# Graph attention with residual norm: the order of the last tiles' powers and stores, the last tile's normalisation, and twelve more stored residuals

## The chip, the cores and the metric

The kernel runs on one core of a Trainium2 chip. The metric is the device time of one execution, in microseconds; lower is better.

## The reference

For 16 batches of 1024 rows of 512 float32 values, the reference computes masked attention with eight heads, adds the input, and normalises every row:

```python
q = (x @ Wq + bq).reshape(b, n, H, HD)          # likewise k, v
scores = jnp.einsum('bqhd,bkhd->bhqk', q, k) / jnp.sqrt(jnp.float32(HD))
scores = scores + (1.0 - adj)[None, None, :, :] * -1000000000.0
attn = jax.nn.softmax(scores, axis=-1)
out = jnp.einsum('bhqk,bkhd->bqhd', attn, v).reshape(b, n, d)
y = x + out @ Wo + bo
result = (y - mean(y)) / sqrt(var(y) + 1e-5)    # over the last axis
```

The adjacency is the same for all batches and sparse: most rows have only a few keys. Rows without any key attend evenly to all of them.

## The kernel before

**Tiles.** Rows are ranked by their number of keys and taken in tiles of 128 rows, eight tiles (`t` from 0 to 7) for a batch `b`; a tile's number is 8b + t. `OWN` gives the number of keys that a tile handles one by one, one *block* for each: 2, 1, 2, 3, 4, 5, 5, 7. Tile 4 of each batch is thus the four-key tile. Rows with more keys than that (tiles 6 and 7) have further blocks, which are added up by a matmul (`add_up`). A block gathers one row of keys and values for each of the 128 queries (`kvg`, an indirect DMA on the queue of GpSimd, which the profile calls POOL), multiplies and reduces on VectorE (DVE), takes exponentials on ScalarE (ACT) and weighs the values on ACT or DVE.

**The schedule.** The program is written out block by block by a planner in Python, in the order in which each engine then works through it. `now[0]` is the step, one for each block. `later(k, fn)` puts a piece of work into the plan of the step k further on, `later_last(k, fn)` into the rest of that step, which comes behind the plan. TensorE (PE) work is paced by a credit: the projections of coming batches (`fronts`) while there are any, and the output products (`finish`) of tiles that are done. `total` is the number of blocks; the steps from `total` on only finish tiles. Each engine, and the DMA queue of each issuing engine (SP issues the plain DMAs), works strictly in the order written.

**A tile's x.** `load_x` gathers the tile's rows of x on POOL (L1010) into one of three buffers; PE transposes them, and the function `out` in `transpose_x` copies the result. For a tile whose number is in `STORED`, SP then writes the gathered rows to a DRAM tensor `residual` (L773), and the load of the tile three further on, which takes the same buffer, is put off by two steps. At the end of a tile, `load_y` needs x again: for a stored tile SP reads `residual` (L1035), for another POOL gathers it once more (L1038).

**The end of a tile.** When its last block is done, `normalise` (DVE) divides by the sum of the exponentials, and `turn` has PE transpose the tile; ACT copies it to `OT` (L1390). `finish` adds the output bias `bo_bc` to y on DVE (L1076), or, in the body of the program for spilled tiles, has a small matmul add it, and has PE do the output product (L799). `complete` then does, in this order: the sum y + product with its row sum (DVE, L1113), the sum of squares about the mean (`spread`, ACT, L1120), `variance` (DVE, L1123), `power`, the inverse square root (POOL, L1126; for two tiles at once L1160), `shift` (DVE, L1129), `norm_out` (ACT, L1134) and `store`, an indirect DMA on POOL (L1138). In the body two tiles share one power instruction, and their steps are put several steps apart. A product that comes back in the last three steps is held until step `total`. In a tile that ends at `total` - 1 or later (`ending`), all the steps follow at once:

```python
            later_last(0 if ending else 1, spread)
            if ending:
                for step in (variance, power, shift):
                    later(1, step)
                later_last(1, norm_out)
```

and `norm_out` puts `store` two steps on with `later(2, store)`. The last tile, `closes[total - 1]`, is tile 6 of batch 15. A pair whose second tile comes in step s has its two shifts and its first `norm_out` in s + 6 and its second `norm_out` in s + 7.

At the very end each engine reads a flag (L1608), which says whether a general version of the kernel has to run in addition; with these inputs it doesn't.

Of the kernel before, what the change touches and what calls it, by code (L numbers as in the profile page):

```python
# [14 lines left out]
OP = mybir.AluOpType  # L15
# [27 lines left out]
LAZY = 2  # L43

SPILL = (*(8 * b + t for b in range(4, 12) for t in (3, 6)), 45, 69, 93, 102, 103, 106, 107)
STORED = {*SPILL, *(i for i in range(10, 102) if i % 8 in (2, 5, 7)), *(i for i in range(102, 128) if i % 8 > 1)}
LATE = 12

AHEAD_LAST = 11
# [129 lines left out]
def kernel(  # L179
# [36 lines left out]
    nc = tc.nc  # L216
    B, N, D = x.shape
# [28 lines left out]
    bo_bc = const.tile([P, D], F32, name="bo_bc")  # L246
# [8 lines left out]
    with ExitStack() as main:  # L255
# [6 lines left out]
        def fill_psum(name):  # L262
            return psum.tile([P, HALF], F32, tag="fill", name=name, bufs=4)
# [80 lines left out]
        def number(b, t):  # L344
            return b * NT + t if t < NT else -1
# [4 lines left out]
        spill = {i: dram.tile([P, D], F32, name=f"spill_{i}") for i in SPILL}  # L350
        residual = {i: dram.tile([P, D], F32, name=f"residual_{i}") for i in sorted(STORED)}
        zeros = work.tile([P, D + HEADS], F32, tag="pv0", name="zeros", bufs=3)
# [93 lines left out]
        now, plan, rest, urgent, known, waiting, combined = [0], {}, {}, [], [], [], []  # L446

        def later(k, fn):
            plan.setdefault(now[0] + k, []).append(fn)

        def later_last(k, fn):
            rest.setdefault(now[0] + k, []).append(fn)
# [170 lines left out]
        shifts, looked = [], []  # L623
# [114 lines left out]
        X, XT, SX, KV, VSUM, NRM, Y, OT, PS = {}, {}, {}, {}, {}, {}, {}, {}, {}  # L738
# [13 lines left out]
        def transpose_x(b, t):  # L752
            def pe():
# [5 lines left out]
                def out():  # L759
# [3 lines left out]
                    if t == 0 and b >= PAIRED_FROM:  # L763
# [7 lines left out]
                        nc.scalar.activation(sq[0:LONE, :], xs[0:LONE, :], AF.Square, accum_out=x_norm[0:LONE, b:b + 1])  # L771
                    if b * NT + t in STORED:
                        nc.sync.dma_start(residual[b * NT + t], xs)  # L773
# [251 lines left out]
        def load_y(b, t, k=None):  # L1025
# [7 lines left out]
            loaded[b, t] = now[0]  # L1033
            if number(b, t) in STORED:
                nc.sync.dma_start(Y[b, t], residual[b * NT + t])  # L1035
# [32 lines left out]
        def finish(b, t):  # L1068


            mean_row = t == ONE_KEY and b >= PAIRED_FROM
            plain = bool(fronts) or mean_row
            biased = not plain and now[0] < total and number(b, t) in (*SPILL, -1)

            if not plain and not biased:
                nc.vector.tensor_tensor(Y[b, t], Y[b, t], bo_bc, op=OP.add)  # L1076

            def out(p):
                OT.pop((b, t))
                if mean_row:  # L1080
                    keep_mean(b, p)
                if not fronts and total - 4 < now[0] < total:
                    later(total - now[0], lambda: complete(b, t, p, plain))
                else:
                    complete(b, t, p, plain)

            units = product(f"po_{b}_{t}", lambda c: OT[b, t][:, ts(c, P)], W["o"], out)
            if biased:
                def bias():
                    nc.tensor.matmul(  # L1090
                        PS[f"po_{b}_{t}"], three.to_broadcast([P, P]), bo_3, start=False, stop=False
                    )

                units.insert(2, (BIAS, bias, None))
            return units

        def complete(b, t, p, plain):
            n, rows, offset = rows_of(b, t)
            y, p = Y[b, t][0:n, :], p[0:n, :]
            ending = not fronts and now[0] >= total - 1  # L1100
            single = fronts or ending or n < P
            if single:
                st = small.tile([P, 5], F32, name="stats", bufs=6)[0:n, :]
            else:

                second = bool(half)
                if not second:
                    half.append([small.tile([P, 2, 5], F32, name="stats_2", bufs=5)])
                st2 = half[0][0]
                st = st2[:, int(second), :]  # L1110
            if plain:
                nc.vector.tensor_tensor(y, p, y, op=OP.add)
            nc.vector.scalar_tensor_tensor(  # L1113
                y, bo_bc[0:n, :] if plain else p, 1.0, y, op0=OP.mult, op1=OP.add, accum_out=st[:, 0:1]
            )

            def spread():

                sq = work.tile([P, D], F32, tag="ysq", name=f"ysq_{b}_{t}", bufs=1)
                nc.scalar.activation(sq[0:n, :], y, AF.Square, bias=st[:, 0:1], scale=-float(D), accum_out=st[:, 2:3])  # L1120

            def variance():
                nc.vector.tensor_scalar(st[:, 2:3], st[:, 2:3], 1.0 / D ** 3, EPS, op0=OP.mult, op1=OP.add)  # L1123

            def power():
                nc.gpsimd.tensor_tensor(st[:, 3:4], st[:, 2:3], neg_half[0:n, :], op=OP.pow)  # L1126

            def shift():
                nc.vector.scalar_tensor_tensor(  # L1129
                    st[:, 4:5], st[:, 0:1], -1.0 / D, st[:, 3:4], op0=OP.mult, op1=OP.mult  # L1130
                )

            def norm_out():
                nc.scalar.activation(y, y, AF.Identity, bias=st[:, 4:5], scale=st[:, 3:4])  # L1134
                later(2, store)

            def store():
                nc.gpsimd.indirect_dma_start(  # L1138
                    out=out_rows[b, t], out_offset=bass.IndirectOffsetOnAxis(ap=rows, axis=0),
                    in_=y, in_offset=None, element_offset=offset,  # L1140
                )
                del Y[b, t]

            later_last(0 if ending else 1, spread)
            if ending:
                for step in (variance, power, shift):
                    later(1, step)
                later_last(1, norm_out)
            elif single:
                late = 1 if fronts else 0  # L1150
                later(2 + late, variance)
                later(3 + late, power)
                later(4 + 2 * late, shift)
                later_last(5 + 2 * late, norm_out)
            elif second:
                later(3, variance)
                mate_shift, mate_norm_out = half.pop()[1]

                def powers():
                    nc.gpsimd.tensor_tensor(  # L1160
                        st2[:, :, 3:4], st2[:, :, 2:3], neg_half[:, :, None].to_broadcast([P, 2, 1]), op=OP.pow
                    )

                def shifts():
                    mate_shift()
                    shift()

                later(4, powers)
                later(6, shifts)
                later_last(6, mate_norm_out)  # L1170
                later_last(7, norm_out)
            else:
                later(3, variance)
                mine = half[0]
                mine.append((shift, norm_out))

                def alone():
                    if half and half[0] is mine:
                        half.pop()
                        power()  # L1180
                        later(2, shift)
                        later_last(3, norm_out)

                later(6, alone)
# [34 lines left out]
        closes = {n: tile_closed for tile_closed, n in closing.items()}  # L1219
# [162 lines left out]
        def turn(b, t, o):  # L1382
            def transpose():
                p = fill_psum(f"poT_{b}_{t}")
                for c in range(NPAIR):
                    nc.tensor.transpose(p[:, ts(c, P)], o[:, ts(c, P)], ident)  # L1386

                def out():
                    OT[b, t] = work.tile([P, D], F32, tag="oT", name=f"oT_{b}_{t}", bufs=LAZY + 2)
                    nc.scalar.copy(OT[b, t], p)  # L1390
                    if number(b, t) in SPILL:
                        later(1, lambda: nc.sync.dma_start(spill[b * NT + t], OT.pop((b, t))))
                        spilled.append((b, t))
                    else:
                        later(1, lambda: done.append((b, t)))

                later(1, out)

            later(1, lambda: urgent.append(transpose))
            if not fronts:  # L1400
                coming.append((b, t))
# [65 lines left out]
        done, coming, spilled, gathered, fronts, guarded = [], [], [], [0], [], []  # L1467

        total = len(blocks)
# [29 lines left out]
        with tc.manual_schedule():  # L1499
# [21 lines left out]
            while n < total or plan or rest or urgent or done or finishing or spilled or lone_tiles or not guarded:  # L1521
# [6 lines left out]
                elif n in start:  # L1528

                    b = start.index(n)  # L1530
# [110 lines left out]
```

## Time and profile before

| | |
|---|---|
| median of 3 runs | 1849.95 us (1849.7 to 1851.8) |
| the profiled execution | 1851.61 us, span 1849.8 us |
| granted TensorE clock, mean | 0.994 |
| busy: PE, DVE, ACT, POOL | 97%, 91%, 85%, 68% |
| DMA | 555.39 MB, mean 300 GB/s |
| residual stores and reads on SP | 71 and 71 |
| gathers of y on POOL (L1038) | 58, 64.1 us busy |
| stores of the output on POOL (L1138) | 129, 150.5 us busy |

The durations in the profile come from one execution, whose own time is some 1.7 us above the median. A line names an instruction by engine, line of the kernel and operation, then output and input. POOLq and SPq are the queues that issue DMAs; "idle before" is the time in which the engine had nothing to do before an instruction, with what released it, where "issue" means that nothing shown held it. The spans on POOL are rough, and a DMA instruction on POOL stands for the work of issuing it, not for the transfer.

### The profile page before, as it was taken

To read this page: it belongs to the slowest core of one execution; us is meant where nothing else is said; L and a number is where in the kernel's file an instruction comes from. 1 tells how busy PE (TensorE), PEld (TensorE's weight loads), DVE (VectorE), ACT (ScalarE), POOL (GpSimd) and SP (SyncE) were. 2 spreads that over 40 slices of the span, in tenths; PEclk is the share of its full clock that TensorE was granted. 3 is DMA by queue.
4 is the path that set the end of the run, shared out by engine and by line. 5 is a ranking of instruction groups with operands and counts; after the bars stand their busy time and mean duration, and the time that the engine had idled before them with its cause. 6 is when DMAs were issued, how large, how long until landed. Compare 5 with 4: busy or idle time off the path is not lost.

```text
span 1849.8 us, 25305 instructions
## 1 busy us (share of the span) xinstructions
PE 1800.1 (97%) x5127; PEld 874.5 (47%) x5140; DVE 1691.9 (91%) x3472; ACT 1565.2 (85%) x6184; POOL 1249.1 (68%) x1154
## 2 busy tenths in 40 slices
PE   7999999999999999999999999999999999999996
PEld 3444454554444454454444445444444444444442
DVE  6889889999989999999999999999999999997885
ACT  3637869989889898999899988999799999977786
POOL 1367866777676686767667676677666777666785
PEclk9999999999999999999999999999999999999998
DMA  7357797988888999989989998998989899898984
GB/s 286 111 186 241 250 326 247 333 303 313 314 285 301 306 319 316 354 302 311 330 311 315 347 311 280 340 327 305 353 304 326 314 347 330 314 326 311 341 312 162
DMA packets 196295, 555.39 MB, mean 300 GB/s; under 512 B 33258, under 2 KB 33278, under 8 KB 196130
## 3 DMA queue, kind: packets, MB, share of 16 engines
q0 software_dynamic: 113600, 373.64, 59.6%
q1 hardware_dynamic: 79454, 174.23, 25.0%
q10 hardware_dynamic: 3076, 5.82, 0.9%
q14 instruction: 122, 1.00, 0.2%
q8 instruction: 43, 0.70, 0.2%
HBM read 420.30 MB, written 154.30 MB: 311 GB/s over the span
## 4 chain that ended last, share of the span: by engine, by line
PE 72%; DVE 11%; DMA 5%; ACT 4%; issue 3%; POOL 1%; SPq 0%; POOLq 0%; DVEq 0%; ACTq 0%
PE po L799 17%; PE pq L799 15%; PE pp L956 13%; PE z L956 9%; PE x L956 9%; ACT pv L1326 2%; PE pxT L757 2%; DVE qk L1298 2%; PE poT L1386 2%; DVE s L1302 2%; PE sum L1352 2%; PE sum L1351 2%; DMA kvg<-kv_pair,place_row 2%; DVE pv L1342 1%; DMA oTs<-spill 1%
## 5 line engine op out<-in xcount | busy, mean ns | idle before, releaser
L1326 ACT ACTIVATE pv<-kvg,pv 128x64 f32<-128x64 f32 x3600 | 907.1, 340 | 0.0
L1277 POOL DMA_INDIRECT kvg<-kv_pair,place_row x462 | 532.2, 1152 | 289.0 <-ACT pv L1326 89.8
L799 PE MATMUL pq<-wq,xT 128*128 128x512 f32 x792 | 368.2, 596 | 0.9 <-DVE q L830 0.9
L1302 DVE TENSOR_REDUCE s<-qk 128x8 f32<-128x512 f32 x530 | 360.6, 680 | 6.7
L799 PE MATMUL po<-wo,oT 128*128 128x512 f32 x792 | 359.2, 593 | 0.2 <-ACT oT L1390 0.2
L1298 DVE TENSOR_TENSOR qk<-qt,kvg 128x512 f32<-128x512 f32 x434 | 296.8, 684 | 4.2 <-DMA kvg<-kv_pair,place_row 3.7
L956 PE MATMUL pp<-t,s 128*128 128x512 f32 x504 | 237.0, 593 | 1.5 <-ACT sq_k L809 1.5
L956 PE MATMUL x<-b,xT 128*128 128x512 f32 x504 | 237.1, 593 | 0.1
L1342 DVE TENSOR_TENSOR pv<-pv,pv 128x520 f32<-128x520 f32 x329 | 228.3, 694 | 4.4 <-ACT pv L1326 4.2
L799 PEld LDWEIGHTS po<-wo,oT 128*128 128x128 f32 x792 | 148.6, 190 | 169.5 <-issue 160.6
L799 PEld LDWEIGHTS pq<-wq,xT 128*128 128x128 f32 x792 | 148.1, 191 | 163.8 <-issue 150.4
L1010 POOL DMA_INDIRECT x<-in_x_dram,asked_row x120 | 136.2, 1135 | 65.8 <-issue 21.2
L1138 POOL DMA_INDIRECT out_dram<-y,asked_row x129 | 150.5, 1166 | 39.6 <-issue 17.3
L1313 ACT ACTIVATE pv<-s,absent 128x8 f32<-128x8 f32 x434 | 126.7, 294 | 54.6 <-DVE s L1302 50.2
L809 ACT ACTIVATE sq_k<-kv 128x128 bf16<-128x128 f32 x512 | 150.8, 300 | 6.1 <-DVE kv L979 3.2
L956 PEld LDWEIGHTS pp<-t,s 128*128 128x128 f32 x504 | 94.3, 190 | 110.1 <-issue 98.4
L956 PEld LDWEIGHTS x<-b,xT 128*128 128x128 f32 x504 | 94.1, 190 | 107.5 <-issue 100.5
L956 PE MATMUL z<-b,s 128*128 128x512 f32 x252 | 120.8, 602 | 6.8 <-DVE kv L984 6.8
L1231 POOL DMA_INDIRECT qg<-q_rows,query_row x96 | 105.4, 1098 | 28.1 <-issue 25.1
L1134 ACT ACTIVATE y<-y,stats 128x512 f32<-128x512 f32 (+1 forms) x129 | 103.6, 806 | 19.0 <-DVE stats L1129 16.1
L956 PE MATMUL z<-t,s 128*128 128x512 f32 x252 | 118.6, 593 | 0.0
L956 PE MATMUL pp<-t,xT 128*128 128x512 f32 x252 | 118.5, 592 | 0.0
(276 smaller groups left out, 2727.7 us busy)
## 6 DMA issues: line engine op xcount, KB each, us to landing
kv_pair<-kv SPq DMA_DIRECT2D x98, 512.0 KB
q_rows<-q SPq DMA_DIRECT2D x106, 256.0 KB
qt<-q_rows SPq DMA_DIRECT2D x98, 256.0 KB
residual<-x SPq DMA_DIRECT2D x71, 256.0 KB
y<-residual SPq DMA_DIRECT2D x71, 256.0 KB
kv_rows<-kv SPq DMA_DIRECT2D x15, 512.0 KB
kvg<-kv_pair,place_row POOLq DMA_INDIRECT x462, 6.6
kv_pair<-kv SPq DMA_DIRECT2D x28, 256.0 KB
```

The source lines that it names most:

```text
L799: nc.tensor.matmul(p, lhs(c), w[:, c, :], start=(c == 0), stop=(c == NPAIR - 1))
L809: nc.scalar.activation(sq, s[:, ts(h, P)], AF.Square, scale=scale, accum_out=sums[:, h:h + 1])
L956: nc.tensor.matmul(R[bank], l[:, ts(c, P)], right[:, c, :], start=(first and c == 0), stop=(c == 1), skip_group_check=True,)
L1010: nc.gpsimd.indirect_dma_start(out=y, out_offset=None, in_=x_rows, in_offset=bass.IndirectOffsetOnAxis(ap=asked_row[:, t:t + 1], axis=0), ...
L1138: nc.gpsimd.indirect_dma_start(out=out_rows[b, t], out_offset=bass.IndirectOffsetOnAxis(ap=rows, axis=0), in_=y, in_offset=None, element_o ...
L1231: nc.gpsimd.indirect_dma_start(out=q, out_offset=None, in_=q_rows[b % ROWS], in_offset=bass.IndirectOffsetOnAxis(ap=rows, axis=0))
L1277: nc.gpsimd.indirect_dma_start(out=KG[n], out_offset=None, in_=rows, in_offset=bass.IndirectOffsetOnAxis(ap=(place_row if b else key_row)[ ...
L1298: nc.vector.tensor_tensor(QK[n], q, KG[n][:, 0:D], op=OP.mult)
L1302: nc.vector.tensor_reduce(S[n], QK.pop(n).rearrange("p (h d) -> p h d", d=HD), axis=AX.X, op=OP.add)
L1313: nc.scalar.activation(PV[n][:, D:], S.pop(n), AF.Exp, bias=bias)
L1326: nc.scalar.activation(pv[:, ts(h, HD)], v[:, ds(D + h * HD, HD)], AF.Copy, scale=pv[:, D + h:D + h + 1])
L1342: nc.vector.tensor_tensor(PV[b, t], PV[b, t], pv, op=OP.add)
```

## The change

Five edits, of which the first touches the body of the program and the others its last steps:

1. `STORED` takes in the four-key tiles 12, 20, ..., 100, twelve in all: their x is written to `residual` by SP and read back, and the load of the tile three further on comes two steps later.
2. A pair completed five steps before `total` has its shifts and both normalisations in step `total`, instead of one and two steps later.
3. In the ending tiles, `shift` goes from the plan of its step into the rest; from step `total` on, `store` comes one step after `norm_out`, in the rest and so behind that step's `power`, instead of two steps after it in the plan.
4. The last tile has `centre` (its mean), `variance` and `power`, and then `last_norm_out`: one VectorE instruction that subtracts the mean and multiplies by the inverse deviation. The store follows at once.
5. The last tile's bias is added in the step of its `OT` copy, instead of in `finish`.

```diff
-STORED = {*SPILL, *(i for i in range(10, 102) if i % 8 in (2, 5, 7)), *(i for i in range(102, 128) if i % 8 > 1)}
+STORED = {*SPILL, *(i for i in range(10, 102) if i % 8 in (2, 4, 5, 7)), *(i for i in range(102, 128) if i % 8 > 1)}
...
-            if not plain and not biased:
+            if not plain and not biased and (b, t) != closes[total - 1]:
                 nc.vector.tensor_tensor(Y[b, t], Y[b, t], bo_bc, op=OP.add)
...
             def norm_out():
                 nc.scalar.activation(y, y, AF.Identity, bias=st[:, 4:5], scale=st[:, 3:4])
-                later(2, store)
+                if not fronts and now[0] >= total:
+                    later_last(1, store)
+                else:
+                    later(2, store)
+
+            def centre():
+                nc.vector.tensor_scalar(st[:, 4:5], st[:, 0:1], 1.0 / D, None, op0=OP.mult)
+
+            def last_norm_out():
+                nc.vector.tensor_scalar(y, y, st[:, 4:5], st[:, 3:4], op0=OP.subtract, op1=OP.mult)
+                store()
...
-            if ending:
-                for step in (variance, power, shift):
+            if ending and (b, t) == closes[total - 1]:
+                for step in (centre, variance, power, last_norm_out):
                     later(1, step)
+            elif ending:
+                later(1, variance)
+                later(1, power)
+                later_last(1, shift)
                 later_last(1, norm_out)
...
                 later(4, powers)
-                later(6, shifts)
-                later_last(6, mate_norm_out)
-                later_last(7, norm_out)
+                shift_at = 6 if fronts else min(6, max(5, total - now[0]))
+                later(shift_at, shifts)
+                later_last(shift_at, mate_norm_out)
+                later_last(7 if shift_at == 6 else 5, norm_out)
...
                     nc.scalar.copy(OT[b, t], p)
+                    if (b, t) == closes[total - 1]:
+                        nc.vector.tensor_tensor(Y[b, t], Y[b, t], bo_bc, op=OP.add)
```

## The prediction

> **What bounds the kernel now.** I read the first rows of the page, then the busy time by stretches, then the order of instructions from 1823 us to the end, then the waits of POOL and SP.
>
> Page, rows 1 and 3 (busy time and instructions; queue, packets, MB, share of the 16 DMA engines):
>
> ```profile
> PE 1800.1 (97%) x5127; PEld 874.5 (47%) x5140; DVE 1691.9 (91%) x3472; ACT 1565.2 (85%) x6184; POOL 1249.1 (68%) x1154
> ...
> q0 software_dynamic: 113600, 373.64, 59.6%
> q1 hardware_dynamic: 79454, 174.23, 25.0%
> ```
>
> Stretches (PE, PEld, DVE, ACT, POOL busy, clock, DMA share, GB/s):
>
> ```profile
> 800.00:1200.00 400.00, 395.63 (x1144) 193.55 (x1145) 378.76 (x738) 358.99 (x1467) 267.65 (x244) 1.00 0.91 317
> ...
> 1830.00:1840.00 10.00, 5.79 (x15) 2.22 (x13) 4.71 (x21) 5.71 (x11) 6.57 (x7) 0.97 0.29 108
> 1840.00:1850.00 10.00, 0.00 (x0) 0.00 (x0) 0.16 (x1) 0.81 (x1) 2.57 (x3) 0.50 0.22 84
> ```
>
> PE fills the body; of the 1650 us from 100 to 1750 it is idle 20.7 us in all. PE's last product ends at 1835.79, so 14 us of the span is tail, where POOL works most. That is where most of the diff lies. The tail in order of time, all engines (start, duration):
>
> ```profile
> 1827.73 0.22 DVE L1129 SCALAR_TENSOR_TENSOR stats<-stats 128x1 f32<-128x1 f32 x2
> ...
> 1831.29 0.56 ACT L1390 COPY oT<-poT 128x512 f32<-128x512 f32 x1
> ...
> 1831.87 0.55 POOL L1126 TENSOR_TENSOR stats<-stats,neg_half 128x1 f32<-128x1 f32 x1 [2.29 <-DVE stats L1123]
> ...
> 1835.20 0.96 POOL L1138 DMA_INDIRECT out_dram<-y,asked_row  x1 [0.30 <-issue]
> 1836.19 0.57 POOL L1126 TENSOR_TENSOR stats<-stats,neg_half 128x1 f32<-128x1 f32 x1
> 1836.80 0.16 DVE L1129 SCALAR_TENSOR_TENSOR stats<-stats 128x1 f32<-128x1 f32 x1 [2.39 <-POOL stats L1126]
> 1836.88 0.69 DVE L1076 TENSOR_TENSOR y<-y,bo_bc 128x512 f32<-128x512 f32 x1
> 1836.95 1.53 POOL L1138 DMA_INDIRECT out_dram<-y,asked_row  x1 [0.19 <-issue]
> 1837.05 0.81 ACT L1134 ACTIVATE y<-y,stats 128x512 f32<-128x512 f32 x1 [2.83 <-DVE stats L1129]
> 1837.67 0.69 DVE L1113 SCALAR_TENSOR_TENSOR y<-po,y 128x512 f32<-128x512 f32 x1
> ...
> 1841.04 0.57 POOL L1126 TENSOR_TENSOR stats<-stats,neg_half 128x1 f32<-128x1 f32 x1
> ...
> 1842.99 1.04 POOL L1138 DMA_INDIRECT out_dram<-y,asked_row  x1 [1.38 <-ACT y L1134]
> ```
>
> Call T the step after the last block, A and B the two tiles completed in it, C, D and E the later ones (E is the last), M and N the older pair whose shifts are the two L1129 at 1827.73. POOL stands idle until 1832.59 apart from powers, then must send the stores of M, A and B before D's power (1836.19). DVE waits at D's shift, and E's bias (L1076) and sum (L1113) stand behind it: the sum comes 1.9 us after PE's product. E's power then waits for two more stores. POOL's queue order, not its work, is late.
>
> **The change part by part.**
>
> *M and N.* Their shifts go from T+1 to T, their ACT normalisations from T+1 and T+2 to T, their stores from T+3 and T+4 to the rest of T+1. N thus joins M ahead of the squares of A and B on ACT. Shifts at 1825.9, M at 1826.15, N at 1826.85 (pitch 0.70, as in the group at 1823.22), squares at 1827.55 and 1828.40 (pitch 0.85, as now), against 1826.69 and 1827.54: 0.9 us later.
>
> *Shifts behind the plan.* DVE now runs variance A, variance B, sum C, shift A, shift B, so it no longer sits out two powers (0.70 and 0.67 us idle now). Powers at 1828.62 and 1829.49, sum C at 1829.33, shift B at 1830.1; ACT normalises A and B at 1830.2 and 1830.9, squares C at 1831.6 and copies E's oT at 1832.3 to 1832.86, 1.0 us later than now. PE waits for this copy: E's product goes from 1832.19 to 1833.2 and ends at 1836.8. This is the price in the tail, and it has no cover.
>
> *Stores one step later instead of two, behind the power of that step.* POOL: M's store 1830.24, N's 1831.5 to 1832.5 (pitch 1.27, as 1833.93 to 1835.20), power C 1832.67 to 1833.24, A's store 1833.43, B's 1834.7 to 1835.66, power D 1835.77, C's store 1836.53, D's (its normalisation ends at 1837.46, and 0.29 passes from ACT to POOL) 1837.8 to 1838.76. What waits behind a power is only stores, for which nobody waits.
>
> *E's bias (0.69 us) with the oT copy*: DVE at 1832.5 instead of 1836.88. Sum E follows PE directly: 1836.85; square, with 1.55 us to its accumulator as now, to 1838.4; variance 1838.43.
>
> *E normalised on DVE.* Power E can start at 1838.78, just after D's store. Then shift (0.16), the ACT pass (0.81) and hops are 1.38 us from power to store now. The new tensor_scalar has a near row:
>
> ```profile
> L361 DVE TENSOR_SCALAR bq_bc<-bq_bc x1: 429/429/429, 9.7 to 9.7; 128x512 f32<-128x512 f32 x1
> ```
>
> With 0.43 for it, 0.05 before and 0.29 after it is 0.77: 0.6 saved. The mean (`centre`, 0.15) lies under the square. Store E starts at 1840.1: 2.9 us earlier than 1842.99.
>
> *A rule against the moved bias.* POOL's power of a pair (L1160) took 0.73 us beside an idle DVE, and 1.70 beside DVE adds with two SBUF inputs:
>
> ```profile
> 1814.80 1.70 POOL L1160 TENSOR_TENSOR stats<-stats,neg_half 128x2 f32<-128x2 f32 x1 [3.41 <-DVE stats L1123]
> ...
> 1821.95 0.73 POOL L1160 TENSOR_TENSOR stats<-stats,neg_half 128x2 f32<-128x2 f32 x1
> ```
>
> The Trainium skill (SBUF — State Buffer, Who interferes with whom) says that such a DVE instruction and a GpSimd instruction reading SBUF shut each other out for a whole instruction. E's bias from 1832.5 to 1833.2 meets power C at 1832.67. With the single power's usual 0.57 the sum is 1840.1; by the rule power C ends 0.6 later, and POOL, then full to its end, hands on about 0.5: 1840.6. The two instructions are expected within 0.2 us of each other and which comes first is open, so I take half: store E at 1840.35, a tail gain of 2.6 us. The same section says that a two-port DVE instruction (an fp32 tensor_scalar) locks GpSimd out of writing descriptors; it could cost at most the 0.43 us of the new instruction, but E's own store is POOL's next work and needs its result, so it costs nothing. Bounds of the tail gain: from power A on POOL has 5 powers of 0.57 and 7 stores at 1.27, 11.7 us of work from 1828.6, so store E cannot start much before 1839.4 (3.6 us). At the other end, one more us on the oT copy and two stretched stores (1.53 against 0.96, 1.1 in all) leave 0.5.
>
> *Four-key tiles: 12 tiles (12, 20, ... 100).* Each adds one residual store on SP (256 KB), moves one x gather of POOL two steps later, and replaces one y gather on POOL by a read on SP. POOL issue: L1038 took 64.1 us for 58, so 12 x 1.105 = 13.3 us less. DMA: the hardware queue used 25.0% of 1849.8 us for 174.23 MB, 2.65 us per MB, or 0.70 us of all engines per tile; the software queue 2.95, or 0.77. So 12 x (0.70 + 0.70 - 0.77) = 7.5 us more DMA time, at a DMA share of 0.91. The moved x load waits on its store, and kvg gathers queue behind it on POOL:
>
> ```profile
> POOL x L1010 <- DMA residual<-x: 6.9, 6, 2.9
> ```
>
> That is 6.9 us in 6 waits, the longest 2.9, over 71 stores, 1.2 us for 12 more, under a prefetch of eight blocks; DVE waited for kvg_pair gathers only 6.4 us in the body, PE for x 0.5 us. On SP the new issues cost about 0.4 us each, 24 x 0.4 = 9.6 us on a queue that mostly waits for q; if a y slot is not free, SP rather than POOL is blocked, with kv and q stores behind (15.8 us in two waits in the body). A pair of tiles takes some 28 us, so an x gather two steps (5.6 us) later still lands (4.9 us) before its transposes. Bounds in PE time: a gain of 2 (a tenth of PE's gaps), a loss of 7.5 (all the DMA time exposed). I take 0: the existing 71 stores coexist with 20.7 us of gaps from all causes. If the cover went, each tile could show its 0.63 us.
>
> **Sum.** The profiled execution took 1851.61 us, with a span of 1849.8. Less 2.6 it is 1849.0, span 1847.2. The median shown is 1.66 below the profiled time, so I carry the difference over: 1849.95 - 2.6 = 1847.3.
>
> **The rivals.**
>
> 1. *The tail as above, and the relieved POOL closes gaps in the body.* For: POOL waits on buffers often and 13.3 us are freed. Against: no PE wait of note names POOL. With 1.5 to 2 us: 1845.5.
> 2. *Slower: the extra stores surface in the body.* Around each of the 12 places a write joins full DMA queues, a kvg or kv transfer comes late, and DVE, with 95% busy, cannot catch up. At the full 7.5 us: 1849.95 - 2.6 + 7.5 = 1854.8. It passes the tail's gain at 0.22 us per tile and 0.2% at 0.53. For: DMA share 0.91. Against: the small waits above, and gathers eight blocks ahead.
> 3. *The new order moves the late point to ACT, and little is won.* N ahead of A's square delays the oT copy by 2 us rather than 1 and the stores stretch: 0.5 won, 1849.4. Against: POOL works off the stores in the meantime anyhow.
>
> **How the numbers follow.** 0.2% is 3.7 us, about what a measurement of this kernel can tell from no change; "faster" begins at 1846.25. Forecast 66% (1845.3 to 1849.3; a third of it beyond the bound, since gaps in the body shift by a us either way): 22 faster, 44 same. Rival 1, 15%, faster. Rival 2, 13%, slower. Rival 3, 6%, same. Together 0.37, 0.50, 0.13. The range from 1843.5 to 1851.5 leaves out most of rival 2 and a twentieth below.
>
> **What would show it.** Right: power D directly after B's store and store C behind it; no shift or ACT pass for E, one DVE instruction of 0.4 us in their place; sum E less than 0.2 us after PE; oT copy of E near 1832.9 less the shift of the body; x from L1038 falling from 58 to 46, residual stores from 71 to 83; last store about 2.6 us earlier against the last block. Wrong: PE idle in the body by over 3 us more or less, or E's product not later although N goes first.

## The result and the profile after

The changed kernel takes 1846.23 us (median of 10 runs, 1842.18 to 1849.28) against 1851.57 us for the kernel before (10 runs, 1849.7 to 1855.9). The ratio is 0.9968, 95% interval 0.9959 to 0.9977: 5.9 us faster, between 4.3 and 7.6. The forecast was 2.6 us, in a range from 1843.5 to 1851.5. The profiled execution, 1842.18 us with a span of 1840.4, was the fastest of the ten, so its span must not be set against the 1849.8 of before without care.

The page of the changed kernel, busy time and DMA queues (columns as before):

```profile
PE 1798.2 (98%) x5140; PEld 876.2 (48%) x5140; DVE 1693.7 (92%) x3473; ACT 1563.2 (85%) x6183; POOL 1215.3 (66%) x1142
...
q0 software_dynamic: 112640, 370.50, 59.3%
q1 hardware_dynamic: 82910, 180.52, 26.2%
```

POOL has 12 instructions fewer (46 y gathers instead of 58), SP writes and reads 83 residuals instead of 71, and the hardware queue moves 6.3 MB more.

The order of time in the tail, around the same instructions as before (start, duration; the kernel's lines have moved, L1148 is the store, L1405 the oT copy, L1407 E's bias, L1144 E's normalisation):

```profile
1817.86 0.17 DVE L1378 TENSOR_TENSOR rden<-sum,pv 128x8 f32<-128x8 f32 x1
...
1819.61 0.22 DVE L1129 SCALAR_TENSOR_TENSOR stats<-stats 128x1 f32<-128x1 f32 x2
...
1823.80 0.69 DVE L1076 TENSOR_TENSOR y<-y,bo_bc 128x512 f32<-128x512 f32 x1
1823.87 1.53 POOL L1148 DMA_INDIRECT out_dram<-y,asked_row  x1 [0.18 <-issue]
...
1825.92 0.56 ACT L1405 COPY oT<-poT 128x512 f32<-128x512 f32 x1
...
1826.13 0.69 DVE L1407 TENSOR_TENSOR y<-y,bo_bc 128x512 f32<-128x512 f32 x1
...
1826.54 3.70 PE L799 MATMUL po<-wo,oT 128*128 128x512 f32 x8 [0.49 <-ACT oT L1405]
1826.69 0.57 POOL L1126 TENSOR_TENSOR stats<-stats,neg_half 128x1 f32<-128x1 f32 x1
...
1830.47 0.68 DVE L1113 SCALAR_TENSOR_TENSOR y<-po,y 128x512 f32<-128x512 f32 x1
1830.54 1.04 POOL L1148 DMA_INDIRECT out_dram<-y,asked_row  x1 [0.18 <-issue]
...
1832.86 0.57 POOL L1126 TENSOR_TENSOR stats<-stats,neg_half 128x1 f32<-128x1 f32 x1
1833.47 0.54 DVE L1144 TENSOR_SCALAR y<-y,stats 128x512 f32<-128x512 f32 x1 [1.12 <-POOL stats L1126]
1834.30 1.04 POOL L1148 DMA_INDIRECT out_dram<-y,asked_row  x1 [0.87 <-DVE y L1144]
```

Two lines of the kernel before that are needed for the comparison are the first instruction of the last tile's normalise and E's output product:

```profile
1824.15 0.17 DVE L1363 TENSOR_TENSOR rden<-sum,pv 128x8 f32<-128x8 f32 x1
...
1832.19 3.60 PE L799 MATMUL po<-wo,oT 128*128 128x512 f32 x8
```

A measure that hardly depends on the body: from the first instruction of the last tile's normalise (1824.15 us in the trace of before, 1817.86 here) to the start of the last store. It is 18.84 us before and 16.44 after, 2.40 us less. In the rest of this text it is called *the tail*. It is nearly the same in every execution of the same order: 18.81 with the old end in another kernel, 16.43 to 16.46 in five more executions with the new one. What follows the last store (5.8 to 6.9 us, in one execution 9.4) varies with no relation to the edits. So of the 5.9 us some 2.4 are the tail and 3.5 (interval 1.9 to 5.2) lie ahead of it, where only the stored tiles differ.

Below, each ratio is to runs of the kernel before in the same session, because in two sessions (that of the halves and `late_turn3`, and that of the four single profiles) every kernel, the one before included, ran some 26 to 28 us slower.

### The profile page after: what moved, and what is told of

The parts are those of the page before. It is cut to its first block, busy times and chain, and to the rows that moved or that the text cites. A ratio compares the mean times of both kernels' runs of the same rounds, so it can differ in the third digit from the quotient of the medians.

```text
span 1840.4 us, 25352 instructions
## 1 busy us (share of the span) xinstructions
PE 1798.2 (98%) x5140; PEld 876.2 (48%) x5140; DVE 1693.7 (92%) x3473; ACT 1563.2 (85%) x6183; POOL 1215.3 (66%) x1142
## 4 chain that ended last, share of the span: by engine, by line
PE 69%; DVE 10%; ACT 9%; DMA 4%; issue 3%; POOL 1%; SPq 0%; POOLq 0%; DVEq 0%; ACTq 0%
PE po L799 17%; PE pq L799 15%; PE pp L956 12%; PE z L956 9%; PE x L956 9%; ACT pv L1341 5%; DVE qk L1313 2%; PE poT L1401 2%; PE pxT L757 2%; PE sum L1367 2%; DVE s L1317 2%; PE sum L1366 2%; DVE pv L1357 1%; ACT sq_k L809 1%; DMA kvg<-kv_pair,place_row 1%
## 5 line engine op out<-in xcount | busy, mean ns | idle before, releaser
L1292 POOL DMA_INDIRECT kvg<-kv_pair,place_row x462 | 526.7, 1140 | 307.4 <-ACT pv L1341 99.6
L1148 POOL DMA_INDIRECT out_dram<-y,asked_row x129 | 146.9, 1139 | 39.1 <-issue 21.2
```

The source lines that it names most:

```text
L1148: nc.gpsimd.indirect_dma_start(out=out_rows[b, t], out_offset=bass.IndirectOffsetOnAxis(ap=rows, axis=0), in_=y, in_offset=None, element_o ...
L1292: nc.gpsimd.indirect_dma_start(out=KG[n], out_offset=None, in_=rows, in_offset=bass.IndirectOffsetOnAxis(ap=(place_row if b else key_row)[ ...
```

## The experiments

### The two halves alone

`tail_only` is the changed kernel with `i % 8 in (2, 5, 7)`; `stored_only` is the kernel before with

```diff
-... if i % 8 in (2, 5, 7)), ...
+... if i % 8 in (2, 4, 5, 7)), ...
```

and `after_again` is the changed kernel beside them.

> All edits at the end, STORED as before. Theory A (the end's edits give 3.1 us, read between the last tile's normalise and the end of the span; the stored tiles give some 2 us in the body): ratio to before 0.9983, span from the last tile's first normalise instruction to the end 22.5 us against 25.65. Rival B (the stored tiles do nothing, the whole 0.32% is the end): ratio 0.9968, which would need an end of under 20 us. Rival C (the body's share is only scatter of the clock): ratio 0.9983, and the stored tiles alone 1.0000.

> Only the four-key tiles' x stored, the end as before. Theory A: ratio 0.9988 (2.2 us), the end 25.6 us as before, and the lead shows at the batches' ends in the trace without half-clock stretches explaining it. Rival C: 0.9998 to 1.0002. My prediction's slower rival: 1.002 or more.

> The changed kernel once more, beside the others on one chip. Theory A: ratio 0.9970, the sum of the two parts. If half-clock stretches behind PE gaps of 2 to 3 us set the scatter, then time falls by about 1.8 us for every 0.001 of mean granted clock within each kernel, and at equal clock the kernels differ by the end's 3.1 us plus what the stored tiles give.

Measured: `tail_only` 0.9988 (0.9973 to 1.0002), `stored_only` 0.9989 (0.9975 to 1.0003), `after_again` 0.9979 (0.9965 to 0.9993). The tails are 16.45, 18.81 and 16.43 us. From the last normalise to the end of the span `tail_only` has 23.3 us, not 22.5, since what follows its last store was 0.7 longer. The three ratios fit theory A, two parts of about 2 us each whose sum is the whole; the single parts have not been resolved from zero, and rival C is weakened by the first comparison (its interval leaves at least 1.9 us for the body) rather than excluded by this one. The changed kernel's own gain is smaller here, 3.9 us (1.3 to 6.6), so the body's share of it, 1.5, is not clear of zero in these runs.

### Which edit shortens the tail

Four kernels, one profile each. `pair_only` is the kernel before with edit 2 alone; the others are the changed kernel with one edit taken back:

```diff
 pair_only (to the kernel before)
-                later(6, shifts)
+                shift_at = 6 if fronts else min(6, max(5, total - now[0]))
+                later(shift_at, shifts)          # and both norm_outs as in the change
 no_pair (to the changed kernel)
-                shift_at = 6 if fronts else min(6, max(5, total - now[0]))
+                shift_at = 6
 act_norm
-                for step in (centre, variance, power, last_norm_out):
+                for step in (variance, power, shift): # then ScalarE, and store() at once
 no_bias
-            if not plain and not biased and (b, t) != closes[total - 1]:
+            if not plain and not biased:         # and no add beside the oT copy
```

> The kernel before with only the pair M and N moved to step T (their stores still two steps after the normalisation). Measure: from the last tile's first normalise instruction to the last store's start on POOL, 18.84 us before and 16.43 to 16.45 in three executions with the changed end. Theory A (the pair's move alone brings POOL's stores of M and N in front of C's power and so empties the queue that held up the powers of D and E): 17.2. Rival B (it is the shorter way from normalisation to store, not in this kernel): 18.5 or more.

> The changed kernel with the pair M and N where it was before (shifts in T+1, normalisations in T+1 and T+2), everything else changed. Theory A: POOL works through three powers and then three stores as before, 17.8 us from normalise to last store. Rival B (store one step after the normalisation does it): 16.5.

> The changed kernel with the last tile's shift on VectorE and its normalisation on ScalarE again, store at once. My prediction's term: 0.6 us, so 17.05 from normalise to last store. Rival: the DVE instruction, 0.54 us in the trace against 0.43 assumed, leaves less, 16.8.

> The changed kernel with the last tile's bias back in its finish, behind D's shift. Theory A (POOL's chain of stores sets E's power, which has 0.4 us to spare on the side of E's sums): 16.6 to 16.7 from normalise to last store. Rival (the sum's delay counts in full): 17.1.

Measured tails: `pair_only` 17.05, `no_pair` 18.12, `act_norm` 17.94, `no_bias` 16.94 us.

The pair is the main edit. Alone it brings 1.79 of the 2.40 us, and without it only 0.72 remain. With the 0.51 of the DVE normalisation (below) that makes 2.30, so the bias and the later shift together leave about 0.1. POOL's queue shows why. In `pair_only`, where `store` still has `later(2, store)`, from the power of A on:

```profile
1852.76 0.58 POOL L1126 TENSOR_TENSOR stats<-stats,neg_half 128x1 f32<-128x1 f32 x1 [0.72 <-DVE stats L1123]
1853.67 0.56 POOL L1126 TENSOR_TENSOR stats<-stats,neg_half 128x1 f32<-128x1 f32 x1 [0.34 <-DVE stats L1123]
1854.41 1.04 POOL L1138 DMA_INDIRECT out_dram<-y,asked_row  x1 [0.18 <-ACT y L1134]
1855.75 0.96 POOL L1138 DMA_INDIRECT out_dram<-y,asked_row  x1 [0.30 <-issue]
1856.73 0.57 POOL L1126 TENSOR_TENSOR stats<-stats,neg_half 128x1 f32<-128x1 f32 x1
```

and in `no_pair`, which has the earlier stores but the pair where it was:

```profile
1850.72 1.11 POOL L1126 TENSOR_TENSOR stats<-stats,neg_half 128x1 f32<-128x1 f32 x2 [0.22 <-DVE stats L1123]
1854.38 0.94 POOL L1126 TENSOR_TENSOR stats<-stats,neg_half 128x1 f32<-128x1 f32 x1 [2.55 <-DVE stats L1123]
1855.51 1.04 POOL L1148 DMA_INDIRECT out_dram<-y,asked_row  x1 [0.18 <-ACT y L1134]
1856.85 0.96 POOL L1148 DMA_INDIRECT out_dram<-y,asked_row  x1 [0.30 <-ACT y L1134]
1858.12 0.96 POOL L1148 DMA_INDIRECT out_dram<-y,asked_row  x1 [0.31 <-issue]
```

Two powers, then the stores of M and N, then the power of C: `pair_only` has POOL's order of the changed kernel. Three powers with 2.55 us of idling and then three stores: `no_pair` has the order of the kernel before. Edit 3's earlier store, one step after the normalisation, moves nothing here: with it taken back from the changed kernel, the written order of all five engines is the same, instruction for instruction. With edit 3's shift taken back instead, only DVE's order differs; no run has this alone.

`act_norm` missed its number because of something else. From E's power to the store it takes 1.95 us (1858.17 to 1860.12), as in `pair_only`, against 1.44 in the changed kernel; this 0.51 is what the DVE instruction saves. The other 0.99 us lie ahead: PE's last product.

```profile
1850.85 5.40 PE L799 MATMUL po<-wo,oT 128*128 128x512 f32 x8 [0.99 <-ACT oT L1406]
```

The same eight matmuls take 3.70 us in the changed kernel's trace, where PE had waited 0.49 us. Here PE had idled twice by about a microsecond (1.02 before a small transpose, 0.99 here), and the granted clock then stood at 0.5 for 3.4 us, from 1851.9 on. Of the 1.70 us that the product takes longer, some 0.5 only fill the time in which E's power waits for POOL in the changed kernel, and 0.2 the time in which E's sum waits there for D's shift; 0.99 are left.

`no_bias` fits neither of its numbers well, 0.50 us lost. E's variance is 0.64 us later against the last normalise (1859.87 against 1844.89, and 1832.20 against 1817.86 in the changed kernel). E's power comes no sooner than POOL is free, and this covers about half of it: by itself the later variance would cost some 0.3 us, if the power starts 0.30 after it as in `act_norm` (an estimate). But POOL is free later still, because of a collision (POOL and DVE of `no_bias`):

```profile
1857.49 0.69 DVE L1076 TENSOR_TENSOR y<-y,bo_bc 128x512 f32<-128x512 f32 x1
1857.56 1.54 POOL L1148 DMA_INDIRECT out_dram<-y,asked_row  x1 [0.18 <-issue]
```

C's store takes 1.54 us beside the bias add and 1.04 in the changed kernel, where E's bias stands elsewhere. This sets the 0.50: E's power starts right behind D's store. The two causes do not add up; without the collision some 0.3 would be left, which is what theory A said.

### Transposes moved off a wait

`late_turn3`: PE idles 3.1 us before the transposes of batch 15's tile 7; here they come two steps later.

```diff
-            later(1, lambda: urgent.append(transpose))
+            later(3 if (b, t) == (B - 1, NT - 1) else 1, lambda: urgent.append(transpose))
```

> The changed kernel with the transposes of batch 15's tile 7 put three steps after its normalise instead of one, so that PE does its next output product first instead of idling 3.1 us for VectorE's o. If that gap and the half-clock stretch behind it (PE clock 0.5 to 0.6 for 3.4 us) are on the path to the end: ratio to before 0.9950 (3 to 4 us faster than the changed kernel). If POOL's chain of powers and stores behind the last normalise sets the end whatever PE does: within 0.5 us of the changed kernel, 0.9968, with PE waiting elsewhere.

Measured: 0.9999 (0.9979 to 1.0020), against 0.9979 for the changed kernel in the same session. The gap stayed, with another name (2.57 us before the `sum` matmul, waiting for DVE's pv), and the tail grew to 19.28 us, since one more tile ended in it. The first number is excluded; against the changed kernel the ratio is 0.0020 higher, some 4 us, which the intervals do not resolve. At this place PE waits for DVE whichever of its works comes next.

### The stored tiles, enlarged and undone

```diff
 unstored (to the changed kernel)
-STORED = {*SPILL, *(i for i in range(10, 102) if i % 8 in (2, 4, 5, 7)), ...}
+STORED = {*SPILL, ...}
 undelayed
                         nc.sync.dma_start(residual[b * NT + t], xs)
-                        later(2, lambda: load_x(n // NT, n % NT))
+                        load_x(n // NT, n % NT)
```

> The changed kernel with no stored tiles among 10 to 101 but the spilled ones: 47 tiles (the twelve four-key tiles and 35 others) gather x twice on POOL and write nothing. An enlargement of the disputed edit. Theory A (a stored tile gives about 2.2/12 = 0.18 us in the body, since POOL has one gather less ahead of the kvg gathers): 8.6 us slower than the changed kernel, ratio to before about 1.002. Rival B (twelve tiles more or less are nothing, the body's share is scatter): as the changed kernel, 0.9975 to 0.998.

> The changed kernel, but the next load into a stored tile's x buffer is issued at once instead of two steps later (all 83 stored tiles). Theory A with POOL's queue as the cause: the gather then stands in POOL's queue waiting for the store to land (about 5 us), with kvg gathers behind; PE waits for DVE and DVE for kvg; 2 to 6 us slower than the changed kernel, ratio about 0.999 to 1.001. Rival (gathers run so far ahead that POOL's waits never show): 0.9975 to 0.998, although POOL's waits for residual stores rise from 20 us to over 100.

Measured: `unstored` 0.9989 (0.9981 to 0.9997), `undelayed` 1.0116 (1.0100 to 1.0131).

`undelayed` is decided: against the changed kernel's 0.9968 it is 27 us slower (1.48% of 1852), far more than either theory said; in its own session it is some 22 us slower than the kernel before. Its waits over the whole span (total, times, longest):

```profile
POOL x L1010 <- DMA residual<-x: 119.2, 25, 8.1
...
DVE qk L1313 <- DMA kvg<-kv_pair,place_row: 30.2, 30, 3.2
```

In the changed kernel the same two waits are

```profile
POOL x L1010 <- DMA residual<-x: 12.4, 9, 2.8
...
DVE qk L1313 <- DMA kvg<-kv_pair,place_row: 1.3, 2, 0.8
```

and in the kernel before 6.9 us (shown in the prediction) and

```profile
DVE qk L1298 <- DMA kvg<-kv_pair,place_row: 6.4, 6, 1.8
```

The x gather waits on POOL for the residual store to land, the kvg gathers queue behind it, and DVE, which is busy 95% of the body, waits for them and can't make it up. The two steps of delay are what keeps a stored tile cheap.

`unstored` is between its two numbers: 0.0021 above the changed kernel, 3.9 us. It takes back 44 tiles, not the 47 of the expectation, since 45, 69 and 93 are spilled tiles and stay stored (83 stores become 39): the twelve four-key tiles and 32 others. That is 0.09 us a tile, less than a third of what the twelve four-key tiles should give each by the body's 3.5 us (0.29), and `unstored` stands where the shorter tail alone would put it (2.4 of 1852 us, 0.9987): by this the other 32 stored tiles give nothing that can be measured. A fixed gain for every stored tile is not the explanation.

The traces of the body tell the two groups apart. DVE's waits for kvg gathers between 300 and 1800 us, summed over the three kinds of gather: 8.7, 6.1, 6.3 and 5.6 us in the four executions without the four-key tiles stored (before, `tail_only`, `unstored`, `pair_only`); 1.3 to 4.6, mean 2.7, in the nine that have them stored with the delay. The difference of the means, 6.7 - 2.7 = 4.0 us, is of the size of the body's gain, and `undelayed` shows the same wait at work with the other sign. That the twelve tiles cause it is shown by the grouping of thirteen executions; that it is the whole gain is argued. No run separates the two ways in which the edit can help, the y gather that POOL no longer issues and the x gather that comes two steps later.

### Filled gaps, and a shorter tail

Half-clock stretches follow some of PE's gaps (below). `fill` puts 11 matmuls (two instructions each in the profile), whose results nobody reads, into four gaps of 2.4 to 3.4 us; `best` adds to this an earlier pair and the bias of C and D by a small matmul:

```diff
 fill (to the changed kernel)
+        FILL, FILL_T = {(5, 0): 2, (10, 0): 3}, {(13, 4): 3, (15, NT - 1): 3}
+        def filler(n, p):
+            for i in range(n):
+                nc.tensor.matmul(p, W["o"][:, 0, 0:P], W["o"][:, 0, :], start=(i == 0), stop=(i == n - 1), ...)
 best (to fill)
-            biased = not plain and now[0] < total and number(b, t) in (*SPILL, -1)
+            biased = not plain and number(b, t) in (*SPILL, -1)
...
+                if not fronts and total - now[0] <= 5:   # shifts and both norm_outs: later_last(4, ...)
...
-                if not fronts and now[0] >= total:
-                    later_last(1, store)
+                if not fronts and now[0] >= total - 1:
+                    later_last(max(1, total + 1 - now[0]), store)
```

> The changed kernel with 11 extra matmuls (0.85 us each, results never read) put where PE stands idle 2.4 to 3.4 us in every execution: before z of batch 5 and 10, before the transposes of tile 4 of batch 13 and of tile 7 of batch 15. They delay nothing by themselves. Theory (a gap of some 2 us or more lets the granted clock fall to half for 3.4 us, 1.7 us lost each time it does): no half-clock stretch at these four places, mean granted clock up by 0.001 to 0.003, 2 to 5 us faster than the changed kernel, ratio 0.995 to 0.997. Rival (the half-clock stretches have another cause, or DVE sets the pace there anyway): ratio as the changed kernel.

> As fill, and at the end: the pair M and N normalised in the rest of step T-1, with their stores still behind the powers of A and B, and the bias of C and D added by a small matmul (0.22 us each) instead of a VectorE add that collides with M's store (1.53 us instead of 0.97). Theory (POOL's chain sets the end): 15.3 us from the last tile's first normalise instruction to the last store, 1.1 less than the changed kernel; ratio to before 0.001 under that of fill. Rival: PE's last product, waiting for the oT copy, sets it, and at most 0.4 us is won.

Measured: `fill` 0.9964 (0.9950 to 0.9977), 1845.87 us, granted clock 0.997 to 0.998 in all five runs, against 0.993 to 0.997 in the ten of the changed kernel. Around z of batch 10, the kernel before, the changed kernel and `fill`:

```profile
1067.97 3.67 PE L956 MATMUL z<-b,s 128*128 128x512 f32 x4 [2.95 <-DVE kv L984]
```

```profile
1065.88 1.98 PE L956 MATMUL z<-b,s 128*128 128x512 f32 x4 [3.01 <-DVE kv L984]
```

```profile
1064.88 2.74 PE L820 MATMUL fl<-wo 128*128 128x512 f32 x6
1067.99 1.98 PE L964 MATMUL z<-b,s 128*128 128x512 f32 x4 [0.38 <-DVE kv L992]
```

The gap is gone, and z takes 1.98 us, where it took 3.67 at half clock in the kernel before. One place in one trace proves little, since the changed kernel's z ran at full clock in its own profile too, behind a gap of 3.01. The count over all traces does: in the twelve without filler 40 of the 60 gaps of over 1.8 us after 300 us are followed by a half-clock stretch within 5 us, while at the eight filled places of `fill` and `best` there is none. So the filler does what it should. But the kernel's time is the changed kernel's within the intervals (0.9964 against 0.9968). The expected 2 to 5 us did not come; a gain of 0.7 or of up to 3 cannot be told apart.

`best` has 0.9958 (0.9944 to 0.9972) and a tail of 15.68 us: 0.76 shorter than the changed kernel, not 1.1. M's store is back at 1.04 us, but the power of C, which now meets E's bias add, takes 0.96 instead of 0.57:

```profile
1832.17 0.69 DVE L1421 TENSOR_TENSOR y<-y,bo_bc 128x512 f32<-128x512 f32 x1
1832.33 0.96 POOL L1134 TENSOR_TENSOR stats<-stats,neg_half 128x1 f32<-128x1 f32 x1
```

It is faster than the kernel before; against the changed kernel its total is not resolved, only its tail.

## Why the prediction was right, and where not

The direction, the range and the tail hold. That the range holds is in part luck: by the first comparison more than half of the 5.9 us comes from a term that the sum had at nothing. Point by point:

- *The tail, 2.6 us:* measured 2.40 (18.84 to 16.44). The bounds 0.5 and 3.6 hold, and so does the reading that POOL would be full to its end: from B's power to E's, only gaps of 0.02 to 0.31 us are left in its queue. E's sum comes 0.23 us behind PE's product instead of 1.9.
- *The pair M and N:* it was priced only as a cost (squares 0.9 us later, oT copy 1.0). In the trace the oT copy is 0.9 us later against the last normalise and E's product 0.6, of which 0.49 show as a wait of PE. But the gain of 1.79 us is the pair's too. The prediction's step "stores one step later instead of two, behind the power of that step" gave the credit to the wrong edit: its timetable had POOL's order right, and the edit that it named leaves this order as it is.
- *E normalised on DVE:* 0.51 instead of 0.6. The instruction took 0.54 us, not the 0.43 of the near row.
- *E's bias:* 0.50 in `no_bias`, set by a collision that the way back brings in; the earlier sum alone is worth some 0.3 (estimated above), since POOL sets E's power in the changed kernel.
- *The rule on two SBUF inputs* of the Trainium skill (SBUF — State Buffer, Who interferes with whom) was weighed at half. The meeting expected, E's bias with the power of C, did not come about: the power started 0.56 us after the bias, when that was nearly done, and took 0.57. Another did: D's bias with M's store, 1.53 us instead of 0.96 to 1.04. That the sum came out at the rule's end (16.45 by it, 16.44 measured) is luck, since the half microsecond was lost at another place than expected. In `best` the expected meeting occurs and costs 0.39.
- *The twelve four-key tiles, 0:* this is the term that was mis-sized. Measured 3.5 us (1.9 to 5.2) by the first comparison less the tail, 2.1 by `stored_only` alone. It was bounded at a gain of 2, from PE's gaps, because no wait of PE names POOL. The path seems to run over DVE: its waits for kvg, 8.7 us in the body before, of which the prediction read one kind (6.4 over the whole span), were taken for too small to matter. PE's idle time from 100 to 1750 us fell from 20.6 to 17.8 us in the two profiles, just inside the 3 us that the prediction gave as a sign of being wrong. Rival 1 had the sign, and its "1.5 to 2 us" was too little. The slower rival is refuted: the added transfers do not surface, although POOL waits longer on residual stores (12.4 us instead of 6.9 at the x gathers, and once 7.2 at a kvg gather).
- *The chance:* more than 0.2% faster came out, which had 0.37; "the same" had 0.50. The error in the body's term is the reason.

What stays open: why twelve four-key tiles bring more than 32 others together, how large the body's gain is (1.5 to 3.5 us in the two sessions, each with a wide interval), and how much of it is DVE's kvg waits. Some of it may pass through the clock: in the session of the halves the mean granted clock was 0.9899 in the 22 runs of the changed kernel and 0.9888 in the 67 of the kernel before.

## What to carry to other kernels

Where an engine works strictly in the written order, write the order out before and after an edit and compare: here the earlier store changed nothing, and moving one older pair by a step gave three quarters of the tail. A load that must wait for a store should be issued late enough that it does not wait at the head of a queue with other loads behind it. A term of "zero, since hidden" should be checked on the engine that is nearly full (DVE at 95%), not only on the one that is fullest.

## What was not expected of the hardware

After a gap of PE of about 2 us or more, the granted clock often stands at half (40 of 60 gaps of over 1.8 us, see `fill`) for some 3.4 us, and 1.7 us of PE time, half of it, go. In the trace of before, three gaps (2.95 us at 1065, 1.88 at 1721, 3.11 at 1812) are followed by such a stretch and three (2.38, 2.67 and 1.96) are not; in that of after only the gap of 3.09 us at 1805 is, of five. In `act_norm` such a stretch came after two gaps of about 1 us each. The Trainium skill (TensorE: Matmul & The Clock Gate, Part 1) has an activity window of about 3.4 us that runs free of the program, which fits that the same gap is punished in one execution and not in the next. It makes the two profiled executions differ by 3.4 us between 100 us and the last normalise (three stretches of 1.7 against one), and over the 10 runs of the changed kernel 0.001 of mean clock goes with 1.7 us (standard error 0.4). Yet `fill`, which removes four places of it, won at most little. Perhaps clock and time go together because both follow from DVE being late; this is argued and not shown.

A VectorE add with two SBUF inputs stretches an output store on POOL from between 0.96 and 1.04 us to 1.53, and a power from 0.57 to 0.96 (`best`). What counts is which starts first. A store that starts 0.07 or 0.08 us behind such an add takes 1.51 to 1.54 us in every trace where this occurs; one that starts 0.2 us or more ahead of the add keeps its 0.96 to 1.04. Beside a DVE instruction that reads one of its inputs from PSUM (po, where the matmuls put their product), the store keeps its time too: C's store in the changed kernel starts 0.07 us behind E's sum (1830.47) and takes 1.04.
